# Three bf16 matmuls without a reader in front of each of three matmul groups of a chunk scan

## The chip, the core and the metric

The kernel runs as one program on one core of one Trainium2 chip. The core has five engines that run side by side and meet only at semaphores: TensorE (PE in the profile, with its weight loads on a row of their own, PEld), VectorE (DVE), ScalarE (ACT), GpSimd (POOL) and SyncE (SP), which issues the DMAs. TensorE reads SBUF and writes PSUM. The metric is the device time of one execution in microseconds (us). A difference of 0.3% of it is about 48 us.

## The reference, cut to what matters

Two layers run over 8 images of 64x64 pixels with 192 channels. Layer 0 projects each pixel to 384 channels, applies a 3x3 depthwise convolution and a silu, and then scans the 4096 pixels in two orders (row by row and column by column, K = 2) with 6 heads of 64 channels and 32 states:

```
da = exp(dt * A);  dtx = dt[..., None] * xh
def step(h, inp):
    da_t, dtx_t, B_t, C_t = inp
    h = da_t[..., None, None] * h + dtx_t[..., None] * B_t[:, :, None, :]
    return (h, einsum('bhpn,bhn->bhp', h, C_t))
y = scan(step, h0, ...) + Ds * xh
```

A gate, an output projection and an MLP follow. Layer 1 is a convolution branch beside a four-direction selective scan with 192 channels and 16 states. The change touches the scan of layer 0 alone.

## The kernel before

Layer 0 of an image is four stages, each a Python generator that records instructions and yields now and then: `conv0` (projection, depthwise convolution, transposes), `ssd` (the scan of layer 0), `mlp0` (gate, output projection, MLP), and what layer 1 needs of it. The selective scan of layer 1 (`selective_scan`) is the outer loop. It goes through 3072 units, 384 for each image. A unit `q` has, in this order on the engines:

- `spread` (L1448): two bf16 matmuls of TensorE into `dB`, a PSUM tile of its own pool with two buffers, recorded one unit ahead;
- `weigh` (L1465): VectorE multiplies `dB` by B;
- `scan` (L1472): VectorE's scan of 1024 steps over `dA` and `dB` into `h`; GpSimd then copies the carry (L1474) and multiplies `h` by C (L1475);
- every fourth unit `gather` (L1486): eight matmuls into `acc`, copied out by ScalarE (L1491).

The stages of the next image's layer 0 are laid beside this loop. The class `Beside` holds them; `half()` is called twice in a unit and advances the current stage by a credit of TensorE microseconds that each `yield` gives as its cost. So one unit lasts as long as its own work and the share of the side stage recorded into it. Image 0 has no scan to stand beside: its layer 0 runs alone in front.

Every instruction is pinned to the order in which it was recorded, so each engine runs its own instructions strictly in that order. Work recorded between two others waits behind the first and holds up the second.

`ssd` works through 32 chunks of 128 positions for each image (two sub-chunks of 64 in two directions). A chunk passes five steps, one chunk apart, by `in_turn`: `fetch` (GpSimd builds `R`, L590), `decays` (transposes into `ps_t`, L604; two sums into `ps_d`, L620, each closed by a bf16 matmul of the constant mask `hide`, L621; ScalarE's exponentials into `M`, L615), `weigh` (`ps_g`, L636; GpSimd's `Hm`, L639, and `xw`, L641; VectorE's product on `M`, L645), `outputs` and `store`. The step `outputs` has the three groups of matmuls that matter here:

- `ps_s` (L656), from `xw`, read by VectorE into `Hm` (L662), from which GpSimd makes `Hn` (L664), to which VectorE adds the other half (L678);
- `ps_h` (L672), from the states `H` and `Hm`, read by VectorE into `yo` (L682);
- `ps_y` (L687), 24 products of 64x64 for the 6 heads, from `M`, on which GpSimd's addition L652 must be done, and `X`; read by VectorE into `yo` (L694).

PSUM tiles come from `cx.one(name)`, which hands out one-bank tiles in rotation: from 4 buffers beside the scan, from 8 while image 0 runs alone. A matmul into a new tile waits until the last reader of that buffer is done. `k["ident16"]` is a 128x128 bf16 identity, `k["hide"]` a 128x64 bf16 mask; both are constants made in `setup`.

## Time and profile before

| | |
|---|---|
| runs | 16043.01 us median of 3 (16030.84 to 16072.04) |
| the profiled execution | 16027.31 us, span 16025.4 us |
| mean granted TensorE clock | 0.854 |
| PE / DVE / ACT / POOL busy | 12969.3 / 12232.0 / 9059.2 / 10981.2 us |
| PE instructions | 69608 matmul records, 69608 weight loads |

The profile's span is the time from the first to the last instruction of one execution; busy times are unions of one engine's instruction records. A matmul record's end is modelled and reaches past its start-to-start spacing, since matmuls are pipelined. An fp32 matmul stands in the trace as two records. The granted clock is the share of TensorE's full rate that a throttle lets through. An engine's idle time is put down to the instruction whose semaphore ended it ("issue" where none is seen).

### The profile page before, as it was taken

Reading aid. Unit: us, or ns where it says so; the run is one execution under the profiler, and the core shown is the slowest. Engines: PE = TensorE matmul, PEld = TensorE weight load, DVE = VectorE, ACT = ScalarE, POOL = GpSimd, SP = SyncE. Lnnn points to the kernel's source line nnn. Section 1 sums busy time; section 2 is a strip of 40 time slices with the busy share of each in tenths; the row PEclk is TensorE's granted clock in tenths of the full one; section 3 lists DMA queues with packets and bytes.
Section 4 is the critical chain, followed back from the end, with each engine's and each line's share of the span. In section 5 each row is a group of like instructions: output and inputs, shape, how many; then the busy total and the mean of one; then the engine's idle time right before and its main releaser. Section 6 shows DMA issues by size and latency. Waiting matters only on the chain. (4 is left out here: it accounts for less than half of the span.)

```text
span 16025.4 us, 207140 instructions
## 1 busy us (share of the span) xinstructions
PE 12969.3 (81%) x69608; PEld 4558.8 (28%) x69608; DVE 12232.0 (76%) x9262; ACT 9059.2 (57%) x13776; POOL 10981.2 (69%) x8165
## 2 busy tenths in 40 slices
PE   8977888789887898778878788787888778877766
PEld 4423322333223322233213332233322333211111
DVE  2268887887778877788678886788867887778994
ACT  3355566555665557655466565664656555655653
POOL 3258776876668766687667876678766776667783
PEclk9987888789887898878978799887988879879887
DMA  3288888878787887978878788887888878888885
GB/s 89 86 213 197 212 206 222 198 206 225 199 227 186 214 221 194 226 187 220 218 199 212 191 221 220 209 213 193 220 208 214 205 197 232 202 228 218 212 217 136
DMA packets 1604247, 3243.11 MB, mean 202 GB/s; under 512 B 389424, under 2 KB 843056, under 8 KB 1603184
## 3 DMA queue, kind: packets, MB, share of 16 engines
q1 hardware_dynamic: 1603184, 3229.84, 79.5%
q8 instruction: 556, 9.11, 0.3%
q14 instruction: 507, 4.15, 0.1%
HBM read 2550.93 MB, written 678.18 MB: 201 GB/s over the span
## 5 line engine op out<-in xcount | busy, mean ns | idle before, releaser
L1475 POOL TENSOR_TENSOR h<-h,bc 128x1024 f32<-128x1024 f32 x3072 | 7239.2, 2357 | 1334.9 <-DVE h L1472 1039.1
L1472 DVE TENSOR_TENSOR_SCAN h<-dA,carry,dB 128x1024 f32<-128x1024 f32 x3072 | 7200.3, 2344 | 479.5 <-ACT dA L1440 152.3
L1465 DVE TENSOR_TENSOR dB<-dB,bc 128x1024 f32<-128x1024 f32 x3072 | 3736.6, 1216 | 1665.2 <-PE dB L1448 1625.0
L1440 ACT ACTIVATE dA<-dA,neg_a 128x1024 f32<-128x1024 f32 x3072 | 3373.9, 1150 | 84.9 <-DMA dA<-dld 78.6
L1486 PE MATMUL acc<-h,gather 128*32 128x512 f32 x12288 | 2169.0, 703 | 319.0 <-POOL h L1475 134.7
L1474 POOL COPY carry<-h 128x1 f32<-128x1 f32 x2304 | 421.6, 183 | 2482.3 <-DVE h L1472 2344.5
L1448 PE MATMUL dB<-dus,spread 48*128 48x512 bf16 x6144 | 1401.2, 433 | 886.1 <-DVE h L1472 842.8
L1491 ACT COPY y<-acc 128x512 f32<-128x512 f32 x1536 | 890.2, 580 | 1842.1 <-issue 1014.9
L884 PE MATMUL ps_c<-p,conv_w 128*96 128x512 f32 x2304 | 1165.5, 628 | 37.3 <-ACT p L904 37.3
L1448 PEld LDWEIGHTS <-spread 48*128 48x128 bf16 x6144 | 321.2, 95 | 2969.5 <-issue 1374.7
L687 PE MATMUL ps_y<-X,M 64*64 64x64 f32 x12288 | 622.2, 277 | 433.3 <-issue 200.1
L336 PE MATMUL ps_cv<-pad,diag 64*64 64x512 f32 x6912 | 852.6, 606 | 19.6 <-ACT y L1491 13.0
L615 ACT ACTIVATE M<-ps_d,ln_dt 128x64 f32<-128x64 f32 x3072 | 666.5, 337 | 275.5 <-PE ps_d L621 206.8
L687 PEld LDWEIGHTS ps_y<-X,M 64*64 64x64 f32 x12288 | 567.7, 186 | 602.2 <-issue 256.5
L1486 PEld LDWEIGHTS acc<-h,gather 128*32 128x32 f32 x12288 | 290.7, 115 | 1223.3 <-issue 522.6
L609 ACT COPY bc<-ps_t 64x256 f32<-64x256 f32 x256 | 93.5, 365 | 917.1 <-PE ps_t L604 917.0
L620 PE MATMUL ps_d<-R,after 128*128 128x384 f32 x1024 | 572.7, 650 | 35.5 <-ACT bc L609 16.1
L1440 ACT ACT_TABLE_LOAD x445 | 570.9, 1283 | 7.9
L884 PEld LDWEIGHTS ps_c<-p,conv_w 128*96 128x96 f32 x2304 | 346.2, 167 | 721.9 <-issue 645.2
L1362 PE MATMUL ps_xp<-u,xp 128*128 128x512 f32 x768 | 471.1, 700 | 92.7 <-DMA u<-u 78.5
L1400 POOL TENSOR_TENSOR du<-dl,u 128x1024 f32<-128x1024 f32 x192 | 452.2, 2355 | 96.2 <-DMA bcd<-rows 81.0
L366 PE MATMUL ps_h<-oa,w1a 128*128 128x256 f32 x1536 | 456.0, 417 | 64.0 <-ACT y L1491 23.3
(248 smaller groups left out, 17979.2 us busy)
## 6 DMA issues: line engine op xcount, KB each, us to landing
dA<-dld SPq DMA_DIRECT2D x3072, 512.0 KB
dud<-terms SPq DMA_DIRECT2D x192, 768.0 KB
dus<-dud SPq DMA_DIRECT2D x1152, 128.0 KB
bc<-bcd SPq DMA_DIRECT2D x256, 512.0 KB
y<-yrows SPq DMA_DIRECT2D x256, 384.0 KB
u<-u SPq DMA_DIRECT2D x192, 512.0 KB
dld<-dl SPq DMA_DIRECT2D x192, 512.0 KB
y<-y SPq DMA_DIRECT2D x3072, 32.0 KB
```

The lines of the kernel that those rows point to most:

```text
L336: pin(nc.tensor.matmul(ps[64 * b : 64 * (b + 1)].rearrange("p (h w) -> p h w", w=WW), lhsT=diag[:, t, :], rhs=pad[64 * i : 64 * (i + 1), b ...
L615: pin(nc.scalar.activation(M[:, d, h, :], ps[:, h * S : (h + 1) * S], AF.Exp, bias=bias))
L620: pin(nc.tensor.matmul(ps, lhsT=k["after"], rhs=flat(R[:, d * NH : (d + 1) * NH, :]), start=True, stop=False))
L687: pin(nc.tensor.matmul(psy[d][here, h * HP : (h + 1) * HP], lhsT=M[here, d, h, :], rhs=X[here, d, h, :], start=True, stop=True,))
L884: pin(nc.tensor.matmul(ps.rearrange("p (h w) -> p h w", w=WW), lhsT=w[:, t, :], rhs=pad[:, dy : dy + RB, dx : dx + WW], start=t == 0, stop ...
L1440: pin(nc.scalar.activation(dAs[q], dAs[q], AF.Exp, scale=k["neg_a"][:, steps[m][1], t, i : i + 1]))
L1448: pin(nc.tensor.matmul(dBs[q][:, half, :], lhsT=k["spread"][here, i % 2, :], rhs=du_of[n][here, i // 2, :], start=True, stop=True,))
L1465: pin(nc.vector.tensor_mul(dBs[q], dBs[q], of(q)[0]))
L1472: pin(nc.vector.tensor_tensor_scan(order(h, g), order(dA, g), order(dB, g), carry, ALU.mult, ALU.add))
L1475: pin(nc.gpsimd.tensor_mul(h, h, C_))
L1486: pin(nc.tensor.matmul(ps[32 * v : 32 * (v + 1)], lhsT=k["gather"], rhs=hs[q - 3 + v][:, here], start=True, stop=True))
L1491: pin(nc.scalar.copy(y[:, here], ps))
```

## The change

A new function inside `ssd` records three matmuls of the mask `hide`, repeated to 384 columns, against the bf16 identity. Each one starts a new sum, so each overwrites the one before, and the first real matmul of the group overwrites the third. It is called with the first of two PSUM tiles of `ps_s`, `ps_h` and `ps_y`, just ahead of the group. No `yield` is added, so the side stage's costs, as `Beside` sees them, stay what they were. Results are unchanged.

```diff
+        def busy(ps):
+
+            for i in range(3):
+                pin(nc.tensor.matmul(
+                    ps[:, : NH * S], lhsT=k["ident16"], rhs=bcast(k["hide"], 1, NH), start=True, stop=True
+                ))
+
         def fetch(c):
...
-            pss = [cx.one("ps_s")[: 2 * N0, :INNER0] for i in range(2)]
+            pss = [cx.one("ps_s") for i in range(2)]
+            busy(pss[0])
+            pss = [ps[: 2 * N0, :INNER0] for ps in pss]
...
             psh = [cx.one("ps_h")[:, :INNER0] for d in range(2)]
+            busy(psh[0])
...
             psy = [cx.one("ps_y")[:, :INNER0] for d in range(2)]
+            busy(psy[0])
```

## The prediction

> **What bounds the kernel now.** I read the page's busy shares and slices, then the stretches in which the chunk scan runs, then who waits there, then one chunk's timeline.

> The page first.

> ```profile
> span 16025.4 us, 207140 instructions
> PE 12969.3 (81%) x69608; PEld 4558.8 (28%) x69608; DVE 12232.0 (76%) x9262; ACT 9059.2 (57%) x13776; POOL 10981.2 (69%) x8165
> PEclk9987888789887898878978799887988879879887
> ```

> No engine is full. TensorE is busiest, and its clock falls to 0.7 to 0.8 once in each image. Cut into stretches (a line: start and end, length, busy us of each engine with its count, clock, DMA):

> ```profile
> 239.00:466.00 227.00, 208.35 (x2594) 109.90 (x2594) 124.13 (x256) 107.69 (x439) 177.44 (x169) 0.94 0.43 116
> 4841.00:5353.00 512.00, 387.71 (x3162) 168.90 (x3162) 415.32 (x427) 257.37 (x607) 422.03 (x357) 0.75 0.76 187
> 7300.00:7700.00 400.00, 354.81 (x1682) 152.60 (x1684) 337.52 (x240) 254.45 (x338) 280.62 (x164) 0.94 0.85 223
> ```

> The first is image 0's chunk scan alone, the second image 3's beside the selective scan, the third is MLP work. The chunk scans of images 1 to 7 take 510 to 531 us each at a clock of 0.74 to 0.76; 511 us for 85 units is 6.0 us a unit, where the whole run averages 16025.4/3072 = 5.2. So this is the slow stage, no engine in it is over 83% busy, and its TensorE runs at half rate for half of the time. Waits in that stretch (us, times, longest):

> ```profile
> PE ps_y L687 <- issue: 28.5, 12, 4.2
> PE ps_s L656 <- POOL xw L641: 24.4, 14, 6.6
> PE ps_y L687 <- DVE Hn L678: 18.7, 9, 3.7
> PE ps_y L687 <- POOL M L652: 12.3, 6, 3.1
> ...
> DVE Hm L662 <- PE ps_s L656: 32.7, 21, 6.8
> DVE Hn L678 <- POOL Hn L664: 28.0, 19, 4.8
> DVE dB L1465 <- PE dB L1448: 19.4, 11, 3.4
> ```

> Two things are to be seen: TensorE idles mostly just ahead of `ps_y` and `ps_s`, where two of the new groups go; and VectorE, which paces the units, waits for TensorE for 32.7 + 19.4 + 5.6 (`ps_y`) + 1.0 (`ps_h`) = 59 of 512 us. The stage is bound by a chain through TensorE, VectorE and GpSimd. Now the same four chunks (20 to 23) in image 5 and in image 6:

> ```profile
> 9057.97:9124.99 67.02, 52.67 (x394) 21.80 (x392) 53.48 (x54) 31.20 (x74) 54.77 (x45) 0.68 0.71 186
> 10984.32:11047.99 63.67, 47.27 (x395) 21.34 (x393) 53.47 (x54) 30.99 (x74) 54.41 (x45) 0.77 0.71 189
> ```

> The same instructions, VectorE and GpSimd busy alike, but the clock is 0.09 higher and the stretch 3.35 us shorter. That is the lever of this change.

> **How the clock is set, by this trace.** The clock record knows two values, 1.0 and 0.5, and changes on a grid of 3.41 us. I counted each window's matmul records in columns: a bf16 column through 128x128 as one, an fp32 record's column as two (384 columns take 0.16 us in bf16, 0.32 in fp32), less in proportion where fewer rows or columns of the array are used. A window at full clock holds 3.41/0.16x384 = 8,190 at most. Of 650 windows under 1,500 the next ran at full clock in 1%; of 1,175 between 1,500 and 3,000 in 40%; of 2,800 above in 99%. The chunk scans of images 1 to 7 stand at 2,590 on average, inside the band that decides.

> **The change, part by part.** In the built program the order on the four other engines is row for row what it was. TensorE gets 256 chunks x 9 = 2,304 matmuls and as many weight loads. The wait for the PSUM buffer moves to the first new matmul; the wait for data (`xw`; `M` and `X`) stays at the real one. Behind them in TensorE's queue stand the real group, then `dB` and `acc` of the selective scan.

> *Price of one.* The same matmul exists, L621:

> ```profile
> 6906.30 0.33 PE L621 MATMUL ps_d<-hide,ident 128*128 128x384 bf16 x1
> 6906.46 0.81 PE L620 MATMUL ps_d<-R,after 128*128 128x384 f32 x2
> ...
> 6924.06 0.53 PE L621 MATMUL ps_d<-hide,ident 128*128 128x384 bf16 x1
> 6924.38 1.38 PE L620 MATMUL ps_d<-R,after 128*128 128x384 f32 x2
> ```

> Start to next start is 0.16 us at full clock, 0.32 at half. Its weight load (98 ns) fits under the matmul before. Three are 0.48 us, a chunk's nine 1.44 us.

> *Image 0 alone.* The steady chunk takes 6.30 us there (`ps_y` at 336.57 and 342.87), almost all at full clock, so there is no clock to gain. `ps_s` starts 0.10 us after TensorE is free, so its three cost 0.38; `ps_h` waits 0.39 us for `Hm` in its middle, which the next three fill but for 0.09; `ps_y` waits about 0.6 us in all, and comes 0.33 late after three groups. GpSimd's `R` then starts late by as much, having waited for `ps_d` already. 31 x 0.33 = +10 us. Ends: 0, and 288 x 0.16 = 46 with no cover.

> *Images 1 to 7, the cost.* At a clock of 0.88 (below) nine take 1.64 us; 224 chunks: 367 us of TensorE time. Cover: per chunk I set each group's length at its clock against the idle time right behind it. Of 62 us an image, 9 lie under waits ahead of `ps_s` and 28 under waits ahead of or inside `ps_y`, which cover `ps_h`'s group too; 39% are uncovered, 143 us. Not all TensorE time reaches the end: going from 0.75 to 0.88 shortens a chunk's 12.1 us of TensorE by 1.8, and by the slope below a chunk by 0.7 to 0.9, so about 0.45. Uncovered time at 0.45 is 64 us; all 367 at 0.45 is 165. I take the middle, 115, since half of the `ps_y` waits are for the PSUM buffer (`Hn`), behind which the new group starts late. The far end is 367, nothing covered.

> *Images 1 to 7, the gain.* A group of three adds 1,152 columns where it stands. Adding that to the windows and reading the next clock from the counted shares (by the present clock, in steps of 500) moves the mean clock from 0.73 (measured 0.75) to 0.86: +0.13, to about 0.88. Were a bf16 column to count 0.7 or 1.5 of what I give it: +0.09 or +0.165. Price of clock: over the 42 stretches of four chunks in images 2 to 7, each compared with the same chunks in other images, a chunk is 7.2 us shorter per unit of clock; over single chunks 5.2. So 224 x 0.13 x 5.2 to 7.2 = 151 to 210 us; I take 180. Ends within this case 105 (0.09, 5.2) and 266 (0.165, 7.2); with no rise, 0.

> *Sum.* -180 + 115 + 10 = -55 on the profiled 16027, 15,972. The median of the runs stands 16 above that execution: 15,988.

> [...] The trace's clock falls in windows in which TensorE works: the stage's 0.75 goes with 387.71 of 512 us busy. [...]

> **Rivals.**
> *Slower: the clock does not rise enough.* Place: the windows around `ps_y`, where TensorE idles for 2 us and then runs 64x64 products; new matmuls that wait for the buffer there come too late to fill them, or the throttle counts something other than columns. Then nine cost 1.44/0.755 = 1.91 us, 427 us for 224 chunks, of which 39% (or 0.45 of all) arrive: 167 to 192, and 10 for image 0: about +180, 16,220. It decides where the rise is under 125/(224 x 6.2) = 0.09, a clock below 0.845. For it: half of the `ps_y` waits are for the buffer. Against: the counted share of 99%.
> *Nothing to be measured.* The chain runs through GpSimd (422 of 512 us) and VectorE (415), and what TensorE gains fills with waits for them, while the new matmuls hide: 16,000 to 16,090. For it: `Hn` waits for GpSimd 28.0 us. Against: the pair of stretches above.
> *More than I take.* Everything hides but 64 us and the clock goes to 0.92: -266 + 64 = -202, 15,841.
> *The change does nothing:* excluded, the matmuls are in the built program.

> **How the numbers follow.** Forecast with its larger variant 0.48, no measurable change 0.22, slower 0.30; a change under 0.3% (48 us) cannot be told here. The forecast's own range is 15,841 to 16,149: -202, and -105 + 165 + 46 = +106, on 16,043. The whole range must take in most of the slower rival: 15,840 to 16,220.

> **What would show it.** The clock of the stretches of images 1 to 7 at 0.84 to 0.92 instead of 0.75, and each 5 to 15 us shorter; image 0's about 10 longer; waits of VectorE for `ps_s` and `dB` shorter, waits ahead of `ps_y` shorter by the new work; all other stages unchanged. I am wrong if the clock there stays under 0.84, if it rises and the chunk does not shorten, or if VectorE's wait for `ps_s` grows.

## The result: the clock rose, and the time did not fall

| | before | after |
|---|---|---|
| median of 20 runs, us | 16033.60 (16010.69 to 16072.04) | 16059.67 (16004.98 to 16083.92) |
| ratio | 1 | 1.0017, 95% interval 1.0010 to 1.0025 |
| profiled execution, us | 16027.31 | 16060.64 |

The changed kernel is slower by 0.17%: 26 us between the medians, where 55 us less were forecast. A loss this small is below the 0.3% that the forecast called measurable, but twenty runs of each tell it from nothing.

The page of the changed kernel, the lines that answer to those of before:

```profile
span 16058.8 us, 211460 instructions
PE 13082.4 (81%) x71912; PEld 4614.7 (29%) x71912; DVE 12232.0 (76%) x9262; ACT 9055.6 (56%) x13776; POOL 10982.1 (68%) x8165
PEclk9988888889888998889978899788998889878887
```

TensorE ran 2,304 more matmuls and was busy only 113 us longer: ten of the 40 slices stood at a clock of 0.7 before, and four do now. Two stretches, image 0's chunk scan alone and image 3's beside the selective scan (start and end, length, busy us of PE, PEld, DVE, ACT and POOL with their counts, clock, DMA):

```profile
238.60:492.10 253.50, 242.06 (x2882) 132.38 (x2882) 125.74 (x256) 108.01 (x439) 178.07 (x169) 0.95 0.39 104
```

```profile
4870.00:5380.00 510.00, 397.45 (x3450) 173.76 (x3450) 415.57 (x427) 256.82 (x607) 422.07 (x357) 0.85 0.76 188
```

Image 3's clock went from 0.75 to 0.85, and its length from 512 to 510 us. Image 0's went from 227 to 253.5. Cut at the same instructions in both traces (an image's chunk scan from its first `R` to its last `yo`), the 33.3 us between the two profiled executions come from three places:

| | before | after | |
|---|---|---|---|
| image 0's chunk scan | 227.7 | 253.5 | +25.8 |
| those of images 1 to 7, sum | 3598.8 | 3594.3 | -4.5 |
| their mean clock | 0.753 | 0.853 | +0.100 |
| everything else | 12198.9 | 12210.9 | +12.0 |

The last row is scatter: over the profiled executions of the kernels below, none of which touches that part, it lies between 12158.8 and 12230.4.

### The profile page after: what moved, and what is told of

It is laid out like the page before. It is cut to its first block, busy times and chain, and to the rows that moved or that the text cites. A ratio compares the mean times of both kernels' runs of the same rounds, so it can differ in the third digit from the quotient of the medians.

```text
span 16058.8 us, 211460 instructions
## 1 busy us (share of the span) xinstructions
PE 13082.4 (81%) x71912; PEld 4614.7 (29%) x71912; DVE 12232.0 (76%) x9262; ACT 9055.6 (56%) x13776; POOL 10982.1 (68%) x8165
## 5 line engine op out<-in xcount | busy, mean ns | idle before, releaser
L1497 PE MATMUL acc<-h,gather 128*32 128x512 f32 x12288 | 2134.5, 693 | 318.1 <-POOL h L1486 137.6
L698 PE MATMUL ps_y<-X,M 64*64 64x64 f32 x12288 | 539.1, 252 | 193.1 <-issue 117.3
L698 PEld LDWEIGHTS ps_y<-X,M 64*64 64x64 f32 x12288 | 488.9, 164 | 306.5 <-issue 187.2
L627 PE MATMUL ps_d<-R,after 128*128 128x384 f32 x1024 | 523.6, 599 | 45.4 <-ACT bc L616 16.1
```

The lines of the kernel that those rows point to most:

```text
L627: pin(nc.tensor.matmul(ps, lhsT=k["after"], rhs=flat(R[:, d * NH : (d + 1) * NH, :]), start=True, stop=False))
L698: pin(nc.tensor.matmul(psy[d][here, h * HP : (h + 1) * HP], lhsT=M[here, d, h, :], rhs=X[here, d, h, :], start=True, stop=True,))
L1497: pin(nc.tensor.matmul(ps[32 * v : 32 * (v + 1)], lhsT=k["gather"], rhs=hs[q - 3 + v][:, here], start=True, stop=True))
```

## The experiments

Two theories stood at the start. A: in images 1 to 7 the higher clock pays for the new matmuls and no more, and the loss is image 0's. C: the new matmuls are hidden, the clock buys nothing, and the two zeros only look like a balance. In the tables "images 1 to 7" is the sum above against the 3598.8 us of before, taken from one profiled execution of each kernel; ratios are of repeated runs, with their 95% interval. The sum has no interval of its own. As a check, the difference between the means of the repeated runs, less image 0's change, comes within 12 us of it in each of the twelve experiments, so differences of 10 to 15 us between two such sums mean little.

### Not in image 0

```diff
-            for i in range(3):
+            for i in range(0 if len(cx.singles) > 1 else 3):
```

(`cx.singles` holds two pools only while image 0 runs alone.)

> The nine new matmuls are recorded only where the chunk scan stands beside the selective scan (images 1 to 7), not in image 0. Theory A (image 0 alone carries the loss, +25.8 us in the profile; images 1 to 7 are even, -4.5 us): image 0's stretch back at 228 us, clock of the other stretches still 0.85, the whole run within 0.1% of the kernel before, ratio 0.9985 to 1.0010. Rival B (the loss lies elsewhere, in the stages behind, which stood 12 us longer): ratio still 1.0010 to 1.0025.

Measured: ratio 0.9999 (0.9990 to 1.0008). Image 0's chunk scan 225.9 us, images 1 to 7 -4.9 us at a clock of 0.851. Theory A holds in this: without image 0's share nothing is left of the loss. Rival B's range was not reached.

### The same TensorE time without the work

```diff
-                    ps[:, : NH * S], lhsT=k["ident16"], rhs=bcast(k["hide"], 1, NH), start=True, stop=True
+                    ps[0:32, : NH * S], lhsT=k["ident16"][0:32, 0:32], rhs=bcast(k["hide"][0:32], 1, NH), start=True, stop=True
```

> The same nine matmuls at the same places with the same 384 columns, but 32 rows by 32 columns of the array instead of 128 by 128, so the same TensorE time with a sixteenth of the counted work. Theory A (the new matmuls cost images 1 to 7 about 140 us and the higher clock gives as much back; the clock follows rows x columns): clock of the stretches stays at 0.74 to 0.77 and images 1 to 7 take 100 to 190 us more than before, the whole run 1.008 to 1.014. Rival C (the new matmuls lie under waits and cost nothing, and the higher clock buys nothing): stretches of images 1 to 7 within 20 us of before in sum, the run 1.001 to 1.003 by image 0 alone. Rival D (the clock follows busy time, not rows x columns): clock 0.83 to 0.87 as in the changed kernel and the same time as it, 1.0017.

Measured: ratio 1.0065 (1.0052 to 1.0077), images 1 to 7 +58.8 us at a clock of 0.775, image 0 258.9 us. Image 3's stretch:

```profile
4902.00:5422.00 520.00, 428.20 (x3448) 180.56 (x3446) 415.64 (x426) 257.11 (x607) 422.11 (x357) 0.78 0.74 184
```

Against the changed kernel's line above, VectorE, ScalarE and GpSimd do the same and TensorE the same number of instructions; only the clock (0.78 for 0.85), TensorE's busy time (428 for 397) and the length (520 for 510) differ. C falls, since the time moved, and D falls, since equal columns at a sixteenth of the array did not lift the clock by the same amount. A's mechanism holds, but at half of the size expected (100 to 190), and the clock rose a little above the range it gave (0.74 to 0.77). The twin is a fair one in TensorE time: from the first new start to the real group's, a thin group takes 0.59 us at full clock and 1.07 at half, a full one 0.58 to 0.59 and 1.07 to 1.10. The two kernels together give both terms, if the time goes in proportion to the clock. The price of the clock: 63.3 us for 0.078, 812 us per unit over 224 chunks, or 3.6 us a chunk. The cost of the nine matmuls at an unchanged clock: -4.5 + 0.100 x 812 = 77 us.

### One group at a time

Only `ps_y`'s call kept, then only `ps_s`'s (image 0 included), then only `ps_h`'s (image 0 left out).

> Only the group ahead of ps_y. Theory A: the low clock sits around ps_y (0.66 to 0.75 at its start, 0.83 to 0.94 at the other two), so this group brings most of the rise: clock of the stretches 0.79 to 0.84, images 1 to 7 together 20 to 80 us shorter than before, image 0 0 to 8 us longer, ratio 0.995 to 1.000. Rival C: 0 plus or minus 20 us.

> Only the group ahead of ps_s. Theory A: it stands where the clock is mostly full already and half of it is uncovered on the way ps_s -> Hm -> Hn: clock of the stretches 0.76 to 0.80, images 1 to 7 together 0 to 50 us longer than before, image 0 5 to 12 us longer, ratio 1.000 to 1.004. Rival C: 0 plus or minus 20 us.

> Only the group ahead of ps_h, and not in image 0. Alone, the ps_s group cost images 1 to 7 27 us and the ps_y group 23, all three together saved 4.5. Theory E (a group pays where idle TensorE time stands right behind it and does not pay where its own buffer or data wait stands ahead of it; ps_h's is the covered one, by the waits of ps_y): clock of the stretches 0.77 to 0.81, images 1 to 7 10 to 50 us shorter than before, ratio 0.997 to 0.9995. Rival F (the three groups only pay together, since the clock needs the whole sum): images 1 to 7 0 to 30 us longer, ratio 1.000 to 1.002.

| three matmuls ahead of | ratio | images 1 to 7 | clock | image 0 |
|---|---|---|---|---|
| `ps_y` | 1.0028 (1.0018 to 1.0039) | +23.4 | 0.797 | 239.8 |
| `ps_s` | 1.0023 (1.0013 to 1.0033) | +27.2 | 0.783 | 236.9 |
| `ps_h` | 1.0008 (0.9999 to 1.0016) | +15.9 | 0.778 | 227.8 |
| all three | 1.0017 (1.0010 to 1.0025) | -4.5 | 0.853 | 253.5 |

Two expectations missed: none of the three pays alone, not even `ps_y`'s, where the clock was lowest, and `ps_y`'s group also cost image 0 12 us where 0 to 8 were expected. The three rises of the clock, 0.044, 0.030 and 0.025, do add up to nearly the whole 0.100; the times do not, +66 against -4.5. The time of the `ps_h` group is the one that rival F expected. Its reason, that the clock needs the whole sum, is not borne out, since the clock rose with each group by itself. Why the times do not add up stays open.

### The same place, more of them

In the `ps_h` version the count was raised to six, nine and twelve.

> The same place with six matmuls instead of three. Theory E: the six take 0.96 us, still under the waits behind (2.1 us a chunk on average in and ahead of ps_y), clock 0.80 to 0.85, images 1 to 7 another 0 to 30 us shorter than with three. Rival F: clock up alike, time like three or longer by up to 40 us.

> Nine matmuls ahead of ps_h, not in image 0: the changed kernel's number of matmuls in a chunk, all at one place. Theory H (the place decides: nine spread over three groups left images 1 to 7 even, since the groups ahead of ps_s and ps_y are not covered): clock 0.85 to 0.88, images 1 to 7 40 to 90 us shorter than before, ratio 0.995 to 0.998. Rival J (the number decides and six is its best): clock alike, images 1 to 7 0 to 30 us shorter, ratio 0.998 to 1.001.

> Twelve ahead of ps_h, not in image 0: 1.9 us of TensorE against waits of about 2.1 us a chunk behind. Clock 0.86 to 0.89. If cover runs out: images 1 to 7 20 to 60 us shorter than before, less than with nine, ratio 0.996 to 0.999. If clock still pays: 60 to 90 shorter, ratio 0.994 to 0.9965.

| ahead of `ps_h`, not in image 0 | ratio | images 1 to 7 | clock |
|---|---|---|---|
| 3 | 1.0008 (0.9999 to 1.0016) | +15.9 | 0.778 |
| 6 | 0.9976 (0.9965 to 0.9987) | -51.6 | 0.839 |
| 9 | 0.9967 (0.9953 to 0.9981) | -59.9 | 0.858 |
| 12 | 0.9968 (0.9955 to 0.9981) | -47.8 | 0.875 |

Six missed theory E's range on the good side: 67 us shorter than with three, where 0 to 30 were expected; rival F, which expected the time of three or longer, falls here. Nine and twelve came out as theory H and "if cover runs out" had it. Nine at one place do what nine at three places do to the clock (0.858 and 0.851, without image 0 in both), and the time is 55 us apart, where only the places differ; by the repeated runs it is 0.9967 against 0.9999. Six, nine and twelve beat both kernels. Nine (15968.14 us median against 16023.26 beside it) and twelve (15969.00 against 16023.64) are the fastest found and cannot be told apart. At twelve the clock still rises and the gain no longer does. Image 3's stretch with nine:

```profile
4817.00:5319.00 502.00, 398.41 (x3450) 174.29 (x3448) 415.32 (x427) 257.99 (x607) 422.86 (x357) 0.86 0.78 190
```

Who waited in it, and in the changed kernel's stretch (us, times, longest). With nine ahead of `ps_h`:

```profile
PE ps_s L664 <- POOL xw L648: 25.7, 14, 7.7
PE ps_y L696 <- issue: 21.7, 10, 3.1
...
PE ps_y L696 <- DVE Hn L687: 6.4, 3, 2.4
PE ps_y L696 <- POOL M L659: 4.7, 6, 1.4
```

In the changed kernel (L585 is the new matmuls' line):

```profile
PE ps_y L585 <- DVE Hn L688: 23.2, 14, 3.7
PE ps_s L665 <- POOL xw L648: 17.5, 9, 7.7
PE ps_y L698 <- issue: 17.0, 7, 3.1
...
PE ps_y L698 <- POOL M L659: 7.3, 6, 1.8
```

With nine at `ps_h`, the wait of `ps_y` for `Hn` is down from 18.7 us in the kernel before to 6.4: the new matmuls stand ahead of that wait and fill part of it. In the changed kernel it is the new matmuls themselves (L585) that wait for `Hn`, 14 times in 32 chunks, for 23.2 us. They stand behind the wait, so that `ps_y` may start only after their own time. That this is what the `ps_y` group costs is argued, not shown: the run that takes the new matmuls out of this wait, below, costs as much.

### All nine ahead of `ps_s`

> All nine matmuls ahead of ps_s, not in image 0. Theory H (the place decides; ps_s feeds Hm, Hn and so VectorE's queue, and half of its chunks have no wait to hide them): clock 0.83 to 0.87 as with nine ahead of ps_h, images 1 to 7 20 to 120 us longer than before where nine ahead of ps_h were 60 shorter, ratio 1.001 to 1.008. Rival J (number and clock decide): 30 to 70 us shorter here too, ratio 0.995 to 0.998.

Measured: ratio 1.0045 (1.0028 to 1.0061), images 1 to 7 +78.3 us at a clock of 0.815. The time is as theory H had it, the clock below its 0.83 to 0.87: the same nine matmuls lift it less here than ahead of `ps_h`. It rose by 0.062 and the time rose too; rival J falls. The two places are 138 us apart, of which the lower clock makes some 35, at 812 us per unit; the rest is the place. Image 3's stretch, and VectorE's waits in it:

```profile
4876.00:5399.00 523.00, 414.76 (x3452) 190.62 (x3448) 413.72 (x426) 257.77 (x607) 422.25 (x357) 0.81 0.74 183
```

```profile
DVE Hm L671 <- PE ps_s L665: 48.0, 23, 8.0
DVE Hn L687 <- POOL Hn L673: 19.1, 13, 4.9
DVE dB L1474 <- PE dB L1457: 14.7, 9, 3.6
```

VectorE's wait for `ps_s` went from 32.7 us to 48.0, and all that stands behind `Hm` in VectorE's queue, the selective scan with it, came later; its waits for GpSimd's `Hn` and for `dB` shrank meanwhile (28.0 to 19.1 and 19.4 to 14.7).

### Past the buffer's wait at `ps_y`

```diff
-            psh = [cx.one("ps_h")[:, :INNER0] for d in range(2)]
+            spare = [cx.one("ps_h") for d in range(2)]
+            psh = [ps[:, :INNER0] for ps in spare]
...
             yield None
+            busy(spare[0])
             ps = pss[1].rearrange("p (h c) -> p h c", c=HP)
             pin(nc.vector.tensor_add(Hn, ps, Hn))
```

with nine matmuls of 128 columns into `ps[:, INNER0:]`, and no other group.

> Not in image 0; nine matmuls of 128 columns (the same 1152 columns) into columns 384 to 511 of the first ps_h tile, which nothing reads, recorded where ps_y's group stood but ahead of VectorE's reading of Hn and ps_h, so that they wait for no buffer. Theory E: the clock rises as with the ps_y group alone (0.79 to 0.82) but the matmuls lie under the wait for Hn, so images 1 to 7 are 10 to 50 us shorter than before, ratio 0.997 to 0.9995; the weight loads of 98 ns make them last up to 0.9 us. Rival G (the cost of the ps_y group is not its wait for the buffer): images 1 to 7 15 to 40 us longer, as with the ps_y group alone.

Measured: ratio 1.0025 (1.0014 to 1.0036), images 1 to 7 +42.8 us at a clock of 0.790. A miss: taken out of the buffer's wait, the work ahead of `ps_y` still cost. The trace of this run shows one thing that it now holds up. In image 3's stretch (518 us) VectorE waits for the new matmuls (L585) before it reads `ps_h`:

```profile
DVE yo L692 <- PE ps_h L585: 18.9, 7, 3.8
```

In the kernel before, VectorE waited there for `ps_h` for 1.0 us. The new matmuls write into the tile that VectorE is about to read. The nine did not last the 0.9 us that the expectation allowed for their weight loads: from the first start to the last there are 0.46 us at full clock, against 0.34 for three of 384 columns. With one more spacing for the last matmul that makes 0.52 and 0.51, an estimate from these two, so the length tells nothing of the cost. How much of it VectorE's wait is was not tried apart.

### The price of the clock at one place

> The six matmuls ahead of ps_h, not in image 0, on 32 rows by 32 columns: their TensorE time without their counted work. With six full ones images 1 to 7 were 52 us shorter than before at a clock of 0.839. Theory H (six under the waits behind cost little, 10 to 40 us; the clock brings 60 to 90): clock 0.75 to 0.78, images 1 to 7 10 to 40 us longer than before, ratio 1.000 to 1.003. Rival I (the six full ones gain in another way than by the clock, by pushing later work into a better order): images 1 to 7 shorter here too, ratio under 0.999.

> Nine ahead of ps_h on 32 rows by 32 columns, not in image 0. Clock 0.77 to 0.80. Against nine full ones (60 us shorter than before at 0.857) this prices the clock at one place with nothing else changed. At 3.6 us per chunk and unit of clock, as between the changed kernel and its thin twin, images 1 to 7 are 50 to 70 us longer than with the full ones (-10 to +10 against before, ratio 0.999 to 1.001); at 2.1, as between the two runs with six, 30 to 45 longer (-30 to -15, ratio 0.998 to 0.9995); at 6.2, the price of the prediction, 90 to 120 longer (+30 to +60, ratio 1.002 to 1.004).

| ahead of `ps_h` | ratio | images 1 to 7 | clock |
|---|---|---|---|
| 9 full | 0.9967 (0.9953 to 0.9981) | -59.9 | 0.858 |
| 9 thin | 1.0005 (0.9991 to 1.0018) | +16.7 | 0.777 |
| 6 full | 0.9976 (0.9965 to 0.9987) | -51.6 | 0.839 |
| 6 thin | 0.9983 (0.9971 to 0.9995) | -27.4 | 0.787 |

Nine thin against nine full, as stretches of image 3; the thin one:

```profile
4861.00:5379.00 518.00, 434.98 (x3450) 190.87 (x3450) 416.40 (x426) 257.09 (x607) 421.13 (x356) 0.77 0.74 185
```

518 us at 0.77 against 502 at 0.86, same counts, same places. Over images 1 to 7 that is 76.6 us for 0.081, 4.2 us per chunk and unit of clock. The pair with six gives 24.2 us for 0.052, 2.1. So the single profiles put the price at 2.1 to 4.2, with the changed kernel's own pair at 3.6. These are no bounds: with nine, the full kernel's profiled execution was the fastest of its seven runs and the thin one's the slowest of its ten. The means of the repeated runs, less image 0's change, put the pairs 69 us apart with nine, 15 with six and 71 for the changed kernel and its twin: 3.8, 1.3 and 4.0. The prediction's 5.2 to 7.2 lies above all of these. The six thin ones went beyond what either theory said: 27 us shorter than before with hardly more clock (0.787) than three full ones (0.778), which were 16 us longer. A share of the gain at `ps_h` is thus not the clock's, as rival I had it, or a stage moves by some 20 us for reasons of alignment whenever something is inserted; this stays open.

## Why the prediction was wrong

**Point by point.** The mechanism was right: the clock of the chunk scans went from 0.753 to 0.853, inside the 0.84 to 0.92 that was to show it, and where the clock alone was taken away, the time rose by 63 us. The sign that was to show the prediction wrong, that the clock "rises and the chunk does not shorten", came true all the same. The sum was wrong in each of its three terms, in the gain and in image 0 to the slow side and in the cost, by less, to the fast side:

| term | forecast | measured |
|---|---|---|
| gain, images 1 to 7 | -180 (0.13 x 224 x 6.2) | -81 (0.100 x 812) |
| cost, images 1 to 7 | +115 | +77 |
| image 0 | +10 | +25.8 |
| sum | -55 | +22 |

The gain and the cost in the last column are worked out from the changed kernel and its twin at 812 us per unit of clock; the two profiled executions were 33.3 us apart, with the +12.0 of everything else.

**The gain was the term that failed.** Two factors were too big. The rise was 0.10 instead of 0.13, near the bound of 0.09 that the count of windows gave; at 6.2 us that makes 42 us of the 99 missing. The larger part is the price, 3.6 us where 6.2 was taken. The price of clock, "over the 42 stretches of four chunks ..., a chunk is 7.2 us shorter per unit of clock; over single chunks 5.2", was read from stretches that were not alike in everything but the clock. Between two executions of the same chunks a longer stretch also spreads the same matmuls over more windows, and in the trace of before the emptier windows are followed by the lower clock (by the prediction's count, the next ran at full clock in 40% of those between 1,500 and 3,000 columns and in 99% of those above); the correlation then counts the consequence as part of the cause. That is an argument. What the trace of before shows is that the slope hangs on where the stretches are cut. Cut at the start of `ps_y`, they give the 7.2 and 5.2 of the prediction; cut at the start of GpSimd's `R`, the same comparison gives 4.6 over four chunks and 2.1 over one, and eleven other instructions of the chunk give 4.5 to 6.8 and 2.3 to 5.7. The cut that was taken gave the highest slope over four chunks. What the runs show is the size, 1.3 to 4.2 when the work in the new matmuls was changed and nothing else. The lower end written for this case, 105, was not low enough.

**Image 0** was thought through step by step, and two steps failed: the price of a group and the cover. TensorE's rows of one steady chunk, before:

```profile
340.09 0.33 PE L621 MATMUL ps_d<-hide,ident 128*128 128x384 bf16 x1
340.35 0.85 PE L656 MATMUL ps_s<-xw,both 64*32 64x384 f32 x8
341.12 0.86 PE L672 MATMUL ps_h<-Hn,bc 32*64 32x384 f32 x4
341.90 0.86 PE L672 MATMUL ps_h<-Hm,bc 32*64 32x384 f32 x4
342.87 1.61 PE L687 MATMUL ps_y<-X,M 64*64 64x64 f32 x48
```

In the changed kernel:

```profile
351.04 0.33 PE L628 MATMUL ps_d<-hide,ident 128*128 128x384 bf16 x1
351.20 0.65 PE L585 MATMUL ps_s<-hide,ident 128*128 128x384 bf16 x3
351.78 0.85 PE L665 MATMUL ps_s<-xw,both 64*32 64x384 f32 x8
352.56 0.66 PE L585 MATMUL ps_h<-hide,ident 128*128 128x384 bf16 x3
353.15 0.54 PE L682 MATMUL ps_h<-Hn,bc 32*64 32x384 f32 x2
...
354.13 0.66 PE L585 MATMUL ps_y<-hide,ident 128*128 128x384 bf16 x3
354.73 1.61 PE L698 MATMUL ps_y<-X,M 64*64 64x64 f32 x48
```

A group of three holds TensorE for 0.58 to 0.60 us (351.20 to 351.78, 352.56 to 353.15, 354.13 to 354.73), not 3 x 0.16 = 0.48: there are 0.10 us between the third and the real group that the price of one did not contain. Ahead of `ps_s` that is the same 0.10 that TensorE stood idle before, and that the prediction took off. It is still there, behind the new matmuls: from the last matmul into `ps_d` to `ps_s` there are 0.74 us where there were 0.26, so the group costs its whole 0.48 and not 0.38. From `ps_s` to `ps_y` there are 2.95 us (351.78 to 354.73) where there were 2.52 (340.35 to 342.87). The two groups in between take 1.19, so the waits cover 0.76 of them, not the 1.0 that was added up from 0.39 and 0.6; the wait for `Hm` inside `ps_h` is gone (its matmuls start 0.19 us behind `Hn`'s instead of 0.78), so the missing quarter lies ahead of `ps_y`. Together that is 0.48 + 0.43 = 0.91 in a chunk instead of 0.33. The chunk's period is 7.20 us instead of 6.30. GpSimd shows where it ends, before and after:

```profile
340.40 1.47 POOL L590 TENSOR_TENSOR R<-upto,da 128x768 f32<-128x768 f32 x1 [0.18 <-PE ps_d L620]
```

```profile
351.35 1.47 POOL L597 TENSOR_TENSOR R<-upto,da 128x768 f32<-128x768 f32 x1 [1.08 <-PE ps_d L627]
```

Its wait for `ps_d` grew from 0.18 to 1.08 us, all of the 0.90.

**The cost** of images 1 to 7 was over-estimated by half, within the bounds given (64 to 165). The reading behind it, that half of the `ps_y` waits are for the buffer, does not stand in the prediction's own lines: there `Hn` ends 18.7 of 59.5 us, a third. In the changed kernel it is 23.2 of 47.5, a half, with the new matmuls in that wait. The other reading, that most of `ps_h`'s work lies under the waits behind it, was right for nine (-59.9 us) and not for three alone (+15.9 us).

**What was to be seen.** Waits of VectorE for `ps_s` and `dB` shrank (32.7 to 29.4, 19.4 to 16.7), `ps_y`'s waits shrank (59.5 to 47.5 us, the new matmuls' own included), the other stages did not move beyond their scatter. The stretches were to be 5 to 15 us shorter each and were 0.6 on average. Of the rivals, "nothing to be measured" is nearest, and the measured median lies in its 16,000 to 16,090. That is luck for its number: it has the new matmuls hidden and the faster clock worth nothing, and against it the thin twin lost 58.8 us, which the faster clock of the full one brought back.

## What to carry to other kernels

Work that has no reader and only keeps a throttled clock up was worth here what its place made of it, as much as its number: nine such matmuls cost 78 us ahead of the group that feeds the pacing engine, evened out when spread over three groups, and saved 60 us ahead of one whose wait comes afterwards. In these runs new work paid only where it stood ahead of a wait and held up nothing that the pacing engine was about to read. And the price of a clock should be measured by changing the clock alone, with a twin that takes the same time and does less work, over repeated runs, not by comparing stretches that happened to run at different clocks.
